# A Mamba scan with side work in hand-chosen slots: half of the pieces stand in other slots

## The chip, the cores and the metric

The kernel runs on one core of one Trainium2 chip. The metric is the device time of one execution in microseconds, as the median of several runs. TensorE is called PE here, VectorE DVE, ScalarE ACT, GpSimd POOL, and SyncE, which issues the DMAs, SP.

## The reference, cut to what matters

A tensor of 8 x 256 x 32 x 32 goes through four layers. The first one is a stack of four Mamba blocks, and the change touches only that; the other three are attention layers. A Mamba block takes the tokens of an image (1024 of 256 channels) and computes:

```python
xn = (xs - mu) * rsqrt(var + 1e-05) * lw + lb
xin, z = split(xn @ iw.T, 2, axis=-1)               # 512 channels each
xin = silu(causal_conv(xin, cw) + cb)               # four taps
proj = xin @ xw.T                                    # 16 for dt, 16 for B, 16 for C
dt = softplus(proj[..., :DTR] @ dw.T + db)
def step(h, t):
    dt_t, b_t, c_t, x_t = t
    h = h * exp(dt_t[..., None] * A) + (dt_t * x_t)[..., None] * b_t[:, None, :]
    return (h, einsum('bdn,bn->bd', h, c_t))         # 16 states a channel
y = ys + xin * dp
xs = xs + y * silu(z) @ ow.T
```

The recurrence over `t` has a state of 512 x 16 values for each image. Everything is float32.

## The kernel before, in words

**Units, steps, slots.** The Mamba phase (`mamba_phase`, L77) cuts the work into 64 units: 4 layers x 8 images x 2 halves of 512 tokens. A unit's scan has 16 steps: two groups `q` of 256 channels, and for each 8 groups `g` of two states. A step has two parts, k = 0 and 1, of 128 channels each. The order of the program is written out by hand. `PARTS` gives it for a step: `ct` (the DMA that spreads C over the partitions, two steps ahead), slot a, `bx0`, `da0`, `y`, `z`, `bx1`, `da1`, slot b, `hc`, slot c, slot d. PE, DVE, ACT and POOL keep this order (class `InOrder`, L40); SP's DMAs are ordered by the scheduler of the framework, which also chooses the buffer of each tile among those of its pool.

What the parts issue:

- `bx0`, `bx1` (`forced` and `state`): 32 matmuls of 64 x 64 on PE form the drive of the recurrence in one of two PSUM buffers `bx`; then DVE runs two scans along the tokens (`TENSOR_TENSOR_SCAN`, the tile `h`). A `bx` buffer is free again when the scans of the part two before have read it.
- `da0`, `da1` (`decays`): ACT computes the decays of the next step, two exponentials each. Eight buffers hold two steps.
- `hc` (`product`): in a first half of the tokens DVE keeps the last column for the second half; POOL multiplies `h` by C.
- `y` (`summed`): PE sums the products of three steps earlier (`LAG_Y`) into PSUM. `z` (`gate`): at the end of a group DVE multiplies the sum by the gate.

**Side work.** The slots a to d carry pieces of other units' work. A unit has 64 slots, four to a step: slot a of step s has number 4s and stands ahead of that step's `bx0`; b, c and d (4s + 1 to 4s + 3) stand behind its `bx1`. On PE the slots 4s + 1 to 4s + 4 lie in one gap between two steps. Five generators hold the side work. `BESIDE_SCAN` says for each which unit it serves, counted from the one that is scanned, and in which slot each of its pieces stands; a slot that stands twice takes two pieces. In a slot the generators are called in the order of the table (`beside`). The pieces are, in order:

- `weights` (two units ahead, in the first unit of a layer only): loads; the exponential of A; a scaled identity; bias matmuls and the scaling of the input weights.
- `onward` (one unit ahead), 16 pieces: `pb`, PE transposes B, ACT copies it to `bt`, and eight small DMAs write it as diagonals to DRAM (`scatter`); then for each of two channel groups the softplus: two matmuls `pd` in two PSUM tiles with two ACT reads each (`e`, `dt`); exponential and `one`; logarithm and `one` again (the logarithm's tile has the tag `sq`, one buffer, which the square of `inward` also has); three POOL additions; the products `dtx` on POOL. The last piece issues nothing.
- `turn` (one unit ahead), 4 pieces: PE transposes `dtx` (`pt`), ACT copies it.
- `outward` (the unit before): load of `xo`; four pieces of output projection on PE (`po`, two tiles, each filled in two pieces), a DVE addition after each tile, and the store. In layer 3 a DVE reduction follows, and after a second half ten more pieces of channel gating (small matmuls `se`, ACT scaling, POOL addition, DVE statistics, loads and stores).
- `inward` (two units ahead), 19 pieces: load of x; mean matmul `pmu` and subtraction on DVE; square on ACT; variance matmul `pvar` with ACT's root; the scaling of `xn` on DVE; then for each of four channel tiles the projection `pin` 0 to 3 with ACT's copy into `xin`, and as a piece of its own three DVE taps of the convolution, which read the same PSUM tile; the gate's projection, `pin` 4 to 7, with ACT's copy `sz`; the SiLU on ACT; and `pp`, the projection to dt, B and C, with its copy and two DMAs.

All of the side work on PE writes PSUM tiles of one pool, `ps_m`, tag `mm`, with two buffers:

```python
ps_b = ctx.enter_context(tc.tile_pool(name="m_psb", bufs=2, space=PSUM))
ps_y = ctx.enter_context(tc.tile_pool(name="m_psy", bufs=1, space=PSUM))
ps_m = ctx.enter_context(tc.tile_pool(name="m_psm", bufs=2, space=PSUM))
```

`DIAGONALS` gives the slots in which a DMA loads one of the next unit's eight diagonals `dg` (L342), which `bx` reads.

Of the kernel before, what the change touches and what calls it, by code (L numbers as in the profile page):

```python
# [52 lines left out]
class Engines:  # L53
# [10 lines left out]
PARTS = ("ct", "a", "bx0", "da0", "y", "z", "bx1", "da1", "b", "hc", "c", "d")  # L64

BESIDE_SCAN = (
    ("weights", 2, (2, 2, 3, 4)),
    ("onward", 1, (3, 5, 8, 12, 12, 13, 21, 25, 27, 31, 35, 35, 41, 46, 46, 51)),
    ("turn", 1, (49, 51, 55, 57)),
    ("outward", -1, (6, 12, 16, 18, 21, 29, 31, 32, 39, 43, 50, 51, 55, 55, 61)),  # L70
    ("inward", 2, (2, 4, 7, 10, 16, 21, 23, 25, 28, 34, 40, 40, 44, 44, 44, 46, 49, 59, 63)),
)

DIAGONALS = (16, 20, 36, 40, 44, 48, 52, 56)


def mamba_phase(tc, ctx, a, spill, ident, gvec, stats):  # L77
# [90 lines left out]
    def out_weights(l, w):  # L168
        w["out"] = wp.tile([P, DT, C], F32, name=f"wo{l}", tag="wo")
        nc.sync.dma_start(w["out"], a["m_out"][l])  # L170
# [171 lines left out]
    def diagonal(s):  # L342

        g = len(s["dg"])
        dg = dgp.tile([P, NB, H, NG], F32, name=f"dg{s['name']}_{g}", tag="dg")
        nc.sync.dma_start(dg, s["dgd"][g * 2 * HALF:(g + 1) * 2 * HALF].rearrange("(p b t j) -> p b t j", p=P, b=NB, t=H))
        s["dg"].append(dg)
# [146 lines left out]
    def beside(n, slot):  # L494

        for what, d, when in BESIDE_SCAN:
# [7 lines left out]
            if slot == when[-1]:  # L504
                for _ in side.pop(what):
                    pass
                if what == "turn" and "out" not in s["w"]:
                    out_weights(s["l"], s["w"])
        if slot in DIAGONALS and 0 <= n + 1 < len(units):
            diagonal(units[n + 1])  # L510
# [609 lines left out]
```

## Time and profile before

| | us |
|---|---|
| median of 3 runs (9191.63 to 9198.40) | 9197.91 |
| the profiled execution, its own time | 9194.97 |
| its span, first to last instruction | 9193.1 |
| PE busy with matmuls, share of the span | 8829.2, 96% |
| DVE busy | 7154.2, 78% |
| POOL busy | 7009.5, 76% |
| ACT busy | 5369.8, 58% |
| mean granted PE clock | 0.975 |

The Mamba phase takes the first 6540 us, some 71% of the span; the rest is attention. In the steady part of the scan, from 211.41 to 6248.59 us, PE is busy 5883.7 us of 6037.2, POOL 5588.2, DVE 5441.1, ACT 4231.0.

In the profile a line names what an instruction writes and reads: `bx<-dg,dtxT` is a matmul that writes `bx`. Nearly all instructions of this phase bear line 48, that of the helper that records them, so they are told apart by their tiles. A float32 matmul shows as two records. An answer on waits says which engine sat idle before which work, and whose end released it. The windows say for a stretch of time how long each engine was busy and which clock PE was granted.

### The profile page before, as it was taken

Reading aid. Unit: us, or ns where it says so; the run is one execution under the profiler, and the core shown is the slowest. Engines: PE = TensorE matmul, PEld = TensorE weight load, DVE = VectorE, ACT = ScalarE, POOL = GpSimd, SP = SyncE. Lnnn points to the kernel's source line nnn. Section 1 sums busy time; section 2 is a strip of 40 time slices with the busy share of each in tenths; the row PEclk is TensorE's granted clock in tenths of the full one; section 3 lists DMA queues with packets and bytes.
Section 4 is the critical chain, followed back from the end, with each engine's and each line's share of the span. In section 5 each row is a group of like instructions: output and inputs, shape, how many; then the busy total and the mean of one; then the engine's idle time right before and its main releaser. Section 6 shows DMA issues by size and latency. Waiting matters only on the chain.

```text
span 9193.1 us, 231133 instructions
## 1 busy us (share of the span) xinstructions
PE 8829.2 (96%) x100850; PEld 4513.2 (49%) x100850; DVE 7154.2 (78%) x7267; ACT 5369.8 (58%) x7646; POOL 7009.5 (76%) x2696
## 2 busy tenths in 40 slices
PE   8999999999999999999999999999799999999998
PEld 4555555555555555555555555555344334434433
DVE  5898988889888898989889999999654554455455
ACT  6667676766776676676667677767323333333334
POOL 5999999999999999999999999999414343343436
PEclk8999999999999999999999999999999999999999
DMA  3434434443443444344444444444200000000000
GB/s 108 129 120 122 124 122 127 121 127 122 122 122 124 127 121 127 122 122 123 123 127 121 137 134 134 135 130 141 99 1 5 10 10 5 5 5 5 1 5 10
DMA packets 559192, 845.58 MB, mean 92 GB/s; under 512 B 311456, under 2 KB 312544, under 8 KB 557536
## 3 DMA queue, kind: packets, MB, share of 16 engines
q1 hardware_dynamic: 558176, 830.71, 29.6%
q8 instruction: 799, 13.09, 0.6%
q14 instruction: 217, 1.78, 0.1%
HBM read 771.31 MB, written 59.24 MB: 90 GB/s over the span
## 4 chain that ended last, share of the span: by engine, by line
PE 86%; DVE 6%; ACT 3%; POOL 2%; issue 2%; DMA 0%; SPq 0%; ACTq 0%; DVEq 0%; POOLq 0%
PE bx L48 20%; PE y L48 19%; PE pin L48 10%; PE fs L655 6%; PE po L48 5%; PE fo L671 4%; DVE h L48 3%; PE fo L759 3%; PE pp L48 3%; PE fs L735 3%; PE pd L48 2%; PE fwq L615 2%; PE fwv L637 2%; PE ft L753 1%; PE pvar L48 1%
## 5 line engine op out<-in xcount | busy, mean ns | idle before, releaser
L48 POOL TENSOR_TENSOR h<-h,ct 128x2048 f32<-128x2048 f32 x1024 | 4640.3, 4544 | 451.9 <-PE y L48 161.3
L48 ACT ACTIVATE da<-dt,A 128x512 f32<-128x512 f32 x4096 | 2642.6, 713 | 224.9 <-DVE h L48 222.6
L48 DVE TENSOR_TENSOR_SCAN h<-da,hc,bx 128x512 f32<-128x512 f32 x2048 | 2456.8, 1261 | 238.8 <-PE bx L48 228.4
L48 DVE TENSOR_TENSOR_SCAN h<-da,bx 128x512 f32<-128x512 f32 x2048 | 2356.9, 1203 | 281.1 <-PE bx L48 266.3
L48 PEld LDWEIGHTS bx<-dg,dtxT 64*64 64x64 f32 x65536 | 1915.0, 135 | 1264.1 <-issue 1178.1
L48 PE MATMUL bx<-dg,dtxT 64*64 64x128 f32 x65536 | 2253.4, 276 | 39.7 <-DVE h L48 28.8
L48 PE MATMUL y<-h,twin 64*64 64x512 f32 x16384 | 2018.8, 608 | 6.1 <-POOL h L48 6.1
L660 ACT ACTIVATE fp<-fs 128x1024 f32<-128x1024 f32 x768 | 765.6, 1022 | 1426.3 <-PE fs L655 1398.0
L48 PE MATMUL pin<-xn,win 128*128 128x512 f32 x2048 | 1009.2, 616 | 61.4 <-ACT sz L48 49.4
L48 PEld LDWEIGHTS y<-h,twin 64*64 64x64 f32 x16384 | 616.1, 138 | 675.6 <-issue 665.8
L677 POOL TENSOR_TENSOR fz<-fz,fp 128x1024 f32<-128x1024 f32 x192 | 478.1, 2490 | 414.5 <-ACT fp L660 410.5
L677 DVE TENSOR_TENSOR fz<-fz,fp 128x1024 f32<-128x1024 f32 x384 | 531.8, 1385 | 328.0 <-ACT fp L660 323.7
L655 PE MATMUL fs<-fq,fk 32*128 32x512 f32 (+1 forms) x3072 | 718.0, 646 | 54.9 <-ACT fp L741 39.3
L48 DVE SCALAR_TENSOR_TENSOR xin<-pin,vec,xin 128x509 f32<-128x509 f32 (+2 forms) x768 | 571.6, 744 | 100.3 <-ACT xin L48 42.8
L671 PE MATMUL fo<-fp,fv 128*32 128x512 f32 (+1 forms) x3072 | 596.6, 615 | 0.0
L48 PEld LDWEIGHTS pin<-xn,win 128*128 128x128 f32 x2048 | 355.6, 191 | 457.9 <-issue 330.4
L48 ACT ACTIVATE xin<-pin,cb,vec 128x512 f32<-128x512 f32 x256 | 199.2, 778 | 621.8 <-PE pin L48 621.8
L48 PE MATMUL po<-sz,wo 128*128 128x512 f32 x1024 | 500.7, 612 | 0.0
L48 ACT ACTIVATE sz<-pin,ib 128x512 f32<-128x512 f32 x256 | 175.9, 687 | 549.8 <-PE pin L48 549.8
L655 PEld LDWEIGHTS fs<-fq,fk 32*128 32x128 f32 (+1 forms) x3072 | 195.3, 185 | 467.8 <-issue 271.0
L677 POOL TENSOR_TENSOR fz<-fp,fp 128x1024 f32<-128x1024 f32 x32 | 83.1, 2597 | 403.2 <-PE fzs L688 240.8
L48 ACT ACTIVATE e<-pd,vec 128x512 f32<-128x512 f32 x256 | 176.1, 688 | 317.4 <-PE pd L48 312.5
(391 smaller groups left out, 8743.4 us busy)
## 6 DMA issues: line engine op xcount, KB each, us to landing
ct<-cdr SPq DMA_DIRECT2D x1024, 512.0 KB, 3.9
dg<-diagonals SPq DMA_DIRECT2D x512, 256.0 KB, 4.3
spill<-xo SPq DMA_DIRECT2D x72, 512.0 KB, 5.3
x<-spill SPq DMA_DIRECT2D x48, 512.0 KB, 7.8
xo<-spill SPq DMA_DIRECT2D x48, 512.0 KB, 5.0
x<-in_x SPq DMA_DIRECT2D x16, 512.0 KB, 8.4
res<-in_x SPq DMA_DIRECT2D x16, 512.0 KB, 5.1
diagonals<-bt SPq DMA_DIRECT2D x512, 4.0 KB, 4.6
```

Source lines behind the costliest of these rows:

```text
L48: return self.tc.keep_in_program_order(getattr(self.engine, name)(*args, **kwargs))
L615: nc.tensor.matmul(ps, lhsT=wt[:, k, m * P:(m + 1) * P], rhs=x[:, k, half * T:(half + 1) * T], start=(k == 0), stop=(k == CT - 1))
L637: nc.tensor.matmul(ps[:, j, :], lhsT=x[:, kc, (t + j) * P:(t + j + 1) * P], rhs=w[f"wv{n}"][:, kc, :], start=(kc == 0), stop=(kc == CT - 1))
L655: nc.tensor.matmul(scs[h // 2][:, h % 2, :], lhsT=k[r:r + D, m, kt * P:(kt + 1) * P], rhs=q[r:r + D, m, half * T:(half + 1) * T], start=Tr ...
L660: nc.scalar.activation(p, scs[j], AF.Exp, scale=scale)
L671: nc.tensor.matmul(acc["o"][r:r + D, :], lhsT=v[:, kt, m * P + r:m * P + r + D], rhs=ps[h // 2][:, h % 2, :], start=(kt == 0), stop=(kt == ...
L677: add(acc["z"][j], acc["z"][j] if kt > 1 else probs[i - 1][j], ps[j], ALU.add)
L735: nc.tensor.matmul(sc[:, half, :], lhsT=q[:, m, t * P:(t + 1) * P], rhs=x[:, m, half * T:(half + 1) * T], start=(m == 0), stop=(m == CT - 1))
L753: nc.tensor.matmul(ps[:, j, :], lhsT=p[:, kt * P:(kt + 1) * P], rhs=dg, start=True, stop=True)
L759: nc.tensor.matmul(po[:, m, :], lhsT=v[:, kt, m * P:(m + 1) * P], rhs=pt[:, kt, :], start=(kt == 0), stop=(kt == TT - 1))
```

## The change

Only the slots change. No instruction is added or taken away: the same pieces of the same generators stand in other slots of a unit.

```diff
 BESIDE_SCAN = (
-    ("weights", 2, (2, 2, 3, 4)),
-    ("onward", 1, (3, 5, 8, 12, 12, 13, 21, 25, 27, 31, 35, 35, 41, 46, 46, 51)),
-    ("turn", 1, (49, 51, 55, 57)),
-    ("outward", -1, (6, 12, 16, 18, 21, 29, 31, 32, 39, 43, 50, 51, 55, 55, 61)),
-    ("inward", 2, (2, 4, 7, 10, 16, 21, 23, 25, 28, 34, 40, 40, 44, 44, 44, 46, 49, 59, 63)),
+    ("weights", 2, (0, 2, 2, 7)),
+    ("onward", 1, (1, 3, 6, 8, 8, 16, 21, 25, 27, 31, 35, 35, 41, 45, 46, 51)),
+    ("turn", 1, (46, 49, 56, 58)),
+    ("outward", -1, (6, 13, 16, 20, 23, 30, 32, 33, 37, 41, 48, 50, 53, 53, 61)),
+    ("inward", 2, (0, 0, 3, 10, 15, 19, 19, 29, 29, 34, 40, 43, 44, 44, 44, 46, 49, 59, 63)),
 )
 
-DIAGONALS = (16, 20, 36, 40, 44, 48, 52, 56)
+DIAGONALS = (12, 20, 36, 40, 44, 48, 52, 56)
```

Read by pieces, the moves with work on PE are these: `pb` from slot 3 to 1 and the first pair of `pd` from 5 to 3 (`onward`); `pmu` from 4 to 0, `pin` 0 from 21 to 19, `pin` 1 from 25 to 29, `pin` 3 from 40 to 43 (`inward`; the taps of `pin` 0 move from 23 to 19, of `pin` 1 from 28 to 29, those of `pin` 2 and 3 stay in 40 and 44); the halves of `po` from 12, 16, 18, 21 to 13, 16, 20, 23; the four `pt` from 49, 51, 55, 57 to 46, 49, 56, 58. Without work on PE: the square from 7 to 3, the scaling of `xn` from 16 to 15; the first group's exponential from 8 to 6, its logarithm from 12 to 8, its POOL additions from 12 and 13 to 8 and 16; the second group's last addition from 46 to 45. The second pair of `pd` stays in slot 27, `pin` 2 in 34, `pin` 4 to 7 in 44, 44, 46 and 49, `pp` in 63.

## The prediction

> **What bounds the kernel now.** I read the busy shares of the page first, then the waits of PE, then the timeline of one unit on PE, and last the clock window by window. The waits, where the columns are the idle time in all, how often, and the longest:
>
> ```profile
> PE pd L48 <- ACT dt L48: 89.5, 63, 1.7
> PE pin L48 <- ACT sz L48: 49.4, 64, 0.8
> ...
> PE bx L48 <- DVE h L48: 28.8, 69, 1.4
> ```
>
> In the scan PE is busy without a break except for these. From the start of unit 1 to the start of unit 61 (211.41 to 6248.59 us) there are 6037.2 us, 100.6 us a unit; PE is idle for 153.5 us of it, 2.56 us a unit: 1.42 before `pd`, 0.78 before `pin`, 0.30 before `bx`. VectorE is busy for 5441 us of that stretch and GpSimd for 5588, so both stand within 10% of PE. The first of the waits looks like this in one unit (start, duration, work, idle time before it):
>
> ```profile
> 3065.09 1.98 PE L48 MATMUL pin<-xn,win 128*128 128x512 f32 x4
> 3067.00 1.12 PE L48 MATMUL pd<-proj,wdt 16*128 16x512 f32 x2
> 3069.53 1.12 PE L48 MATMUL pd<-proj,wdt 16*128 16x512 f32 x2 [1.42 <-ACT dt L48]
> 3070.59 1.90 PE L48 MATMUL bx<-dg,dtxT 64*64 64x128 f32 x32
> 3072.24 2.84 PE L48 MATMUL y<-h,twin 64*64 64x512 f32 x16
> ```
>
> The second `pd` waits until ScalarE has read the first one. And what follows the wait is slower than elsewhere: `bx` takes 1.90 us for what takes 1.10 in other steps, `y` 2.84 for 1.90. The windows around it say why. Columns: length, busy us of PE, PEld, DVE, ACT, POOL, then the granted clock, DMA share and GB/s.
>
> ```profile
> 3063.90:3067.31 3.41, 3.41 (x41) 1.78 (x34) 3.38 (x5) 1.10 (x3) 3.25 (x4) 1.00 0.51 185
> 3067.31:3070.73 3.42, 2.00 (x8) 0.44 (x10) 3.38 (x4) 1.88 (x4) 3.42 (x3) 1.00 0.19 44
> 3070.73:3074.14 3.41, 3.41 (x44) 2.24 (x45) 2.38 (x4) 3.41 (x6) 3.41 (x2) 0.50 0.82 268
> 3074.14:3077.55 3.41, 3.41 (x88) 2.31 (x84) 2.44 (x3) 3.38 (x5) 1.86 (x1) 1.00 0.14 31
> 3091.21:3094.62 3.41, 2.63 (x7) 1.02 (x6) 3.41 (x5) 0.69 (x1) 3.41 (x1) 1.00 0.09 29
> 3094.62:3098.03 3.41, 3.41 (x51) 1.58 (x53) 3.34 (x5) 2.51 (x5) 3.41 (x3) 1.00 0.62 176
> ```
>
> The window with the 1.42 us of idle time is followed by one at half clock; the one with the 0.78 us before `pin` (fifth line) is not. I laid all clock records of the scan on this grid of 3.41 us: in units 1 to 60 there are 60 stretches at half clock, 279.9 us in all (38 of one window, 22 of two), nearly all beginning within 2.2 us of the second `pd`. Of the windows of the whole trace with 1.4 to 1.5 us idle 56 of 58 were followed by half clock, of those with 0.7 to 0.8 none of 65. So the wait costs twice: 1.42 us, and 279.9 / 2 / 60 = 2.33 us a unit for matmuls at half speed. Together 3.75 us of 100.6.
>
> [...]
>
> **The change part by part.** Times are from the start of a unit's first `bx`, medians over 16 units from the timelines.
>
> *The second delta pair.* Before, `pin` 1 (slot 25, read by VectorE until slot 28) held one bank when the two `pd` of slot 27 came, so both got the other: in the built order the pair shares a bank in 63 units of 63. After, `pin` 1 comes in slot 29, and the pair shares a bank in 1 unit. Each then waits for readers that are long done: the first for `pin` 0's, at about 31 us, the second for the `xo` addition at about 36.5, while PE arrives at 39. This takes away 1.42 + 2.33 = 3.75 us a unit. What is late next stands below.
>
> *`pin` 1 and its taps in slot 29.* VectorE now works off the three taps (2.22 us without overlap) after step 7, and `pin` 2's at slot 40 after step 9; step 9 has no side work on PE behind it. Let E be the end of `pin` 1. ScalarE's copy lets the taps begin at E + 0.9 (before: `pin` 0 ends at 37.08, taps at 37.98). Then 2.22 for the taps, 4.69 for step 8 (26.72 to 31.41 in a step without a wait), 2.33 for the first two scans of step 9, and 0.1 to PE: E + 10.2. PE, unhindered, needs step 8 (3.63), `pin` 2 (1.91) and step 9 without side work (3.53) and wants that `bx` buffer at E + 9.0. **A new wait of 1.2 us before `bx` of step 10**, each unit. Bounds: 0 if VectorE's chain is shorter than I laid it, 2.0 where VectorE comes in late, as in layer 3, where a reduction of 1.22 us is added at slot 23.
>
> Does that trip the clock? Windows with only `bx` and `y`:
>
> ```profile
> 6415.78:6419.19 3.41, 1.66 (x41) 1.23 (x39) 2.75 (x4) 3.27 (x6) 3.41 (x2) 1.00 0.11 36
> 6419.19:6422.60 3.41, 2.78 (x48) 1.43 (x48) 1.15 (x2) 0.25 (x1) 3.41 (x2) 1.00 0.56 195
> 6477.22:6480.63 3.41, 2.06 (x65) 1.65 (x61) 3.41 (x4) 1.45 (x2) 3.08 (x1) 1.00 0.47 183
> 6480.63:6484.05 3.42, 2.89 (x60) 1.65 (x52) 3.42 (x4) 2.17 (x3) 1.75 (x1) 1.00 0.75 225
> ```
>
> Idle times of 1.75 and 1.35 us there left the clock at 1.00; 2.12 (at 6443 us) did not. With `pd`, which fills 16 of 128 rows, 1.09 was enough and 1.04 was not. So 1.2 us before a `bx` should leave it.
>
> *`pb` and the first delta pair (slots 3, 5 to 1, 3).* They now follow each other on PE, and the second `pd` takes `pb`'s bank: a new wait for ScalarE's copy `bt`. Queued behind it on PE are the `bx` of step 1, and so VectorE. Before, `bt` ended 1.08 us after `pb` (5.12 against 4.04), since ScalarE was still at decays. After, `pmu` (1.92 us) stands ahead on PE while ScalarE's row of work from `pt` 3 is the same 12.0 us plus its copy, 12.6 in all, against 13.05 on PE to the end of `pb`: ScalarE is there first, `bt` ends 0.25 us after `pb`, and the first `pd` covers 0.53. I take 0; upper bound 1.08 - 0.53 = 0.6.
>
> *`pmu` and subtraction to slot 0, square to 3.* The matmul and the 1.2 us of VectorE lie beside `pp` and cost nothing: VectorE stands at about -2 then. The load of x is issued a unit ahead in SP's order in both kernels, now before the eight writes of the diagonals rather than after them; the next `ct` behind them needs 3.9 us to land and has two products of 4.5 us on GpSimd as cover.
>
> *Logarithm to slot 8.* It shares a buffer with the square, so on ScalarE it now waits for the `pvar` matmul, and the decays of step 3 queue behind it. `pvar` ends near 14.2; logarithm and identity take 2.1, the first decay is there at 17.0; VectorE wants it at 17.35. Cost 0, and up to 0.3 on VectorE, which has 2.8 us before PE asks for that buffer.
>
> *GpSimd's sums (12, 13, 46 to 8, 16, 45).* The sum of its work is 16 x 4.50 + 14.2 + 5.0 + 2.0 = 93.2 us a unit, under 98. Laid in the new order, its products end 2.3 us or more before their `y`. Cost 0; without that cover the first late one would be step 12's.
>
> *The rest.* `po` 0 and 1 in slots 13, 16, 20, 23, the transposes in 46, 49, 56, 58 and `pin` 3 in 43 are the same matmuls beside the same steps; `pin` 4 and 5 share a bank in 63 units as before, so 0.78 stays. The first diagonal moves from slot 16 to 12, but stands directly behind the writes in SP's order in both. The weights' pieces act in 4 units of 64. I take 0 for all.
>
> *Sum.* A unit: 100.6 - 3.75 + 1.2 = 98.1. Gain 2.55 x 62 units = 158 us; less 0.8 x 13 units of layer 3, and a half-clock window in some of them (13 x 0.9), 22 us together: 136. The profiled execution took 9194.97 us (span 9193.1), 2.9 under the median of 9197.91. 9194.97 - 136 = 9059, with 3 us to the median 9062; the start, where matrix sums no longer stand behind the weights' load (8.9 us of waiting), should give some back: **9055**.
>
> **The rivals.** (A) The new waits trip the clock once a unit as the old one did: 98.1 + 2.33 = 100.4, 13 us gained in all, 9185. For it: the fit of two windows to a threshold is thin. Against: the lines above. 0.10. (B) Slower: the second `pd` of slot 3 waits for `bt` because ScalarE doesn't get ahead. [...] 98.1 + 1.1 + 2.33 = 101.5, 0.9 x 62 = 56 us lost, 9250. For it: 1.08 us of lag before. Against: `pmu` on PE ahead of it. 0.08. (C) The new VectorE wait doesn't come: 96.9 a unit, 62 x 1.2 more gained, 8980. 0.10. That the bank conflict stays is excluded by the built order (1 of 63).
>
> **How the numbers follow.** The likeliest case, 9055 with 8990 to 9120 (new wait 0.6 to 1.8 us), has 0.72. The range of 8965 to 9160 adds (C) and leaves out (B) and most of (A). About 0.2% (18 us) is what a measurement of this kernel can tell from no change. Faster by more than that: 0.72 + 0.10 + 0.03 of (A) = 0.85; within: 0.07; slower: 0.08.
>
> **What would show it.** Right: no wait of `pd` on `dt`, a mean clock above 0.98, no half-clock window a unit, waits of `bx` on `h` of some 60 to 80 us instead of 28.8, `pin` on `sz` still near 49. Wrong: half-clock windows behind `bx` of step 10 (A), waits of `pd` on `bt` (B), or waits of `y` on GpSimd's `h`, which would mean that GpSimd, not VectorE, is late next.

## The result, and the profile after

The kernel after took **8987.25 us** (median of 4 runs, 8978.97 to 8989.28) against 9197.44 for the kernel before (4 runs, 9191.63 to 9198.40). The ratio is 0.9771, with a 95% interval of 0.9754 to 0.9788: 210 us gained, where 142 were forecast. The time lies in the forecast range of 8965 to 9160, but 68 us under its number, 9055, and 3 us under the 8990 that bounded its likeliest case. The profiled execution took 8988.71 us, its span 8986.9, and the mean granted clock is 0.990 (before: 0.975).

The waits of PE after, by the same view as before (idle time in all, how often, the longest):

```profile
PE bx L48 <- DVE h L48: 93.0, 134, 4.9
PE pin L48 <- ACT sz L48: 49.7, 65, 0.8
...
PE pd L48 <- ACT dt L48: 2.2, 1, 2.2
```

The 89.5 us of `pd` on `dt` are 2.2, from one occurrence; the wait of `pin` on `sz` is what it was; `bx` waits for VectorE 93.0 us instead of 28.8. Here are the second delta pair and the new wait in one unit (start, duration, work, idle time before it):

```profile
3066.03 1.13 PE L48 MATMUL pd<-proj,wdt 16*128 16x512 f32 x4
3067.09 1.10 PE L48 MATMUL bx<-dg,dtxT 64*64 64x128 f32 x32
3068.01 1.90 PE L48 MATMUL y<-h,twin 64*64 64x512 f32 x16
...
3083.06 1.10 PE L48 MATMUL bx<-dg,dtxT 64*64 64x128 f32 x32 [1.00 <-DVE h L48]
```

Three things are to be seen. The four records of the pair stand together and take 1.13 us, as much as *two* of them took before (1.12). The `bx` and `y` behind them take 1.10 and 1.90 us, and the granted clock is 1.00 from 3066.20 to 3069.62. And `bx` of step 10 waits 1.00 us. The clock windows around the new wait (length, busy us of PE, PEld, DVE, ACT, POOL, then clock, DMA share, GB/s):

```profile
3079.87:3083.28 3.41, 2.41 (x55) 1.45 (x49) 3.38 (x5) 3.38 (x6) 3.41 (x2) 1.00 0.15 55
3083.28:3086.69 3.41, 3.41 (x81) 2.25 (x73) 3.34 (x5) 2.77 (x5) 3.41 (x3) 1.00 0.57 196
```

The first has the 1.00 us of idle time, the next one is at clock 1.00.

From the start of unit 1 to that of unit 61 there are now 5832.3 us, 97.21 a unit (before 100.62). PE is idle in 138.3 us of it (before 153.5): 85.8 before `bx`, 46.7 before `pin`, none before `pd`. Half-clock stretches are left at the three layer changes alone, 13.7 us where there were 279.9 in all (6.8 of them at layer changes). So a unit gained 3.41 us, of which only 0.25 is idle time; the rest, 98.06 less 94.90 = 3.16 us, is time in which PE was busy before. Half clock explains (279.9 - 13.7) / 2 / 60 = 2.22 of it, an estimate that takes half of the time at clock 0.50 as lost. **What the other 0.94 are, my sum had no term for**, and this is what the experiments went after.

### The profile page after: what moved, and what is told of

Same layout as the page of the kernel before. It is cut to its first block, busy times and chain, and to the rows that moved or that the text cites. A ratio compares the mean times of both kernels' runs of the same rounds, so it can differ in the third digit from the quotient of the medians.

```text
span 8986.9 us, 231646 instructions
## 1 busy us (share of the span) xinstructions
PE 8635.8 (96%) x100850; PEld 4454.0 (50%) x100850; DVE 7164.6 (80%) x7267; ACT 5375.6 (60%) x7646; POOL 6999.4 (78%) x2696
## 4 chain that ended last, share of the span: by engine, by line
PE 80%; DVE 11%; ACT 3%; issue 3%; POOL 2%; DMA 1%; SPq 0%; POOLq 0%; DVEq 0%; ACTq 0%
PE bx L48 17%; PE y L48 16%; PE pin L48 9%; DVE h L48 8%; PE fs L655 6%; PE po L48 5%; PE fo L671 5%; PE fo L759 3%; PE fs L735 3%; PE pp L48 3%; PE fwq L615 2%; PE fwv L637 2%; PE pd L48 2%; PE pvar L48 1%; PE ft L753 1%
## 5 line engine op out<-in xcount | busy, mean ns | idle before, releaser
L48 PEld LDWEIGHTS bx<-dg,dtxT 64*64 64x64 f32 x65536 | 1886.6, 133 | 1303.3 <-issue 1048.8
L48 PE MATMUL bx<-dg,dtxT 64*64 64x128 f32 x65536 | 2224.0, 273 | 119.7 <-DVE h L48 93.0
L48 PE MATMUL y<-h,twin 64*64 64x512 f32 x16384 | 1958.3, 591 | 4.8 <-POOL h L48 4.8
L48 PE MATMUL pin<-xn,win 128*128 128x512 f32 x2048 | 991.6, 612 | 64.5 <-ACT sz L48 49.7
L48 POOL TENSOR_TENSOR e<-e,one 128x1024 f32<-128x1024 f32 x128 | 303.7, 2372 | 78.6 <-ACT one L48 78.6
```

The source lines that it names most:

```text
L48: return self.tc.keep_in_program_order(getattr(self.engine, name)(*args, **kwargs))
```

## The experiments

Unless another number of runs is given, each was timed with four executions beside the kernel before, whose median was 9190.8 to 9195.4 us. A unit means the mean of units 1 to 60.

**Only `pin` 1 moved**: the kernel before with

```diff
-    ("inward", 2, (2, 4, 7, 10, 16, 21, 23, 25, 28, 34, ...
+    ("inward", 2, (2, 4, 7, 10, 16, 21, 23, 29, 29, 34, ...
```

> The kernel before with one move alone: pin 1 and its taps from slots 25 and 28 to 29 and 29. In the built order the second pair of pd no longer shares a bank (1 unit of 63), all other pieces stand as before. Bank theory: the wait (1.42 us), the half clock (2.2 us) and the lost overlap of the two pd (about 1.0 us) go in each of some 61 units, and pin 3 stays in slot 40, so that the gap on PE behind step 9 is filled and no wait of bx on h of 1 us appears: 9197 - 4.6 x 61 = about 8915. Rival, that the changed kernel gains from all of its moves together: this one move gives at most half of the 210 us, about 9090 or more.

Measured: 9001.89 us (9000.27 to 9006.15), ratio 0.979 [0.9774, 0.9806]. So one of the many moves carries 193 of the 210 us. PE is busy 94.94 us a unit, as in the kernel after, and half clock is down to 13.7 us: the gains came in full. But the time is 87 us above the 8915 that I expected, for there is a new wait of PE in front of step 7, 56.7 us in all, where I had expected none:

```profile
2973.15 1.13 PE L48 MATMUL pd<-proj,wdt 16*128 16x512 f32 x4
2975.22 1.10 PE L48 MATMUL bx<-dg,dtxT 64*64 64x128 f32 x32 [0.95 <-PE pd L48]
```

The releaser named there is PE's own `pd`, which had ended 0.94 us before. VectorE's timeline at the same time shows the real one:

```profile
2970.44 2.32 DVE L48 SCALAR_TENSOR_TENSOR xin<-pin,vec,xin 128x509 f32<-128x509 f32 x3 [1.29 <-ACT xin L48]
2972.68 8.30 DVE L48 TENSOR_TENSOR_SCAN h<-da,hc,bx 128x512 f32<-128x512 f32 x7
```

The scans of step 6 begin at 2972.68 and the second of them, which frees the `bx` buffer, ends about 2975.1. I took the idle time of 1.29 us at the head of the taps of `pin` 0, ahead of these scans, for the cause of the lateness; that isn't shown, and the last experiment doesn't settle it. In the kernel before, the taps have the same 1.29 us, but PE stood before `dt` then, and the lateness cost nothing.

**Only `pin` 1 left where it was**: the kernel after with

```diff
-    ("inward", 2, (0, 0, 3, 10, 15, 19, 19, 29, 29, 34, ...
+    ("inward", 2, (0, 0, 3, 10, 15, 19, 19, 25, 28, 34, ...
```

> The changed kernel with pin 1 and its taps put back to slots 25 and 28, all other moves kept. The pair of pd shares a bank again in 63 units. Bank theory: wait, half clock and lost overlap return (4.6 us a unit), the new wait of bx on h (1.0 us) goes: 8987 + 3.6 x 61 = about 9205, level with before. Rival, that the other moves carry part of the gain: clearly under before, 9100 or less.

Measured (9 runs): 9224.09 us (9211.08 to 9239.76), ratio 1.0028 [1.0018, 1.0038]. The wait before the second `pd` is back with 85.3 us in these units, half clock with 273 us. All the other moves together, without this one, make the kernel 0.28% slower: PE is busy as long as before (98.07 a unit) and idle 0.48 us longer; of these 29 us in 60 units, 24 are before `bx` of step 10.

**Both `pd` of a pair on the same rows**: the kernel after with

```diff
-                nc.tensor.matmul(pds[r], lhsT=w["dt"][r * H:r * H + DTR, i * P:(i + 1) * P], rhs=tokens(proj[r * H:r * H + DTR, :]),
+                nc.tensor.matmul(pds[r], lhsT=w["dt"][:DTR, i * P:(i + 1) * P], rhs=tokens(proj[:DTR, :]),
```

The rows 64 to 79 hold a second copy of the same projection and of the same weights, made so that the two `pd` of a pair, which differ in their channels, can stand on different rows. So the values stay what they are, and the work is the same in number and shape.

> The changed kernel with both pd of a pair on the same 16 rows, so that they run one after the other instead of side by side; they compute the same. Nobody waits for a bank. Overlap term: 0.95 us for each of two pairs a unit, 8987 + 2 x 0.95 x 61 = about 9103. If only idle time trips the clock, it stays at full speed in all but some 3 windows; if rows count, [...] some units may lose up to 2 us more (up to 9200). If the overlap is worth nothing: level with 8987.

Measured: 9039.17 us (9033.13 to 9049.25), ratio 0.9834 [0.9818, 0.985]; 52 us slower than the kernel after, half of what I expected. The second pair, which took 1.13 us:

```profile
2110.84 1.98 PE L48 MATMUL pd<-proj,wdt 16*128 16x512 f32 x4
2112.75 1.00 PE L48 MATMUL bx<-dg,dtxT 64*64 64x128 f32 x28
```

From `pd` to `bx` there are 1.91 us instead of 1.06. That is the missing term: a `pd` on rows 0 to 15 and one on rows 64 to 79 of PE ran side by side in the kernel after, 1.06 us against 1.91 on the same rows. Before, with one bank (one buffer of `ps_m`) for the pair, they couldn't, since the second `pd` waited 1.42 us until ScalarE had read the first. The other half of my expectation failed because the *first* pair lost only 0.16 us: it took long already. In the kernel after, it stands directly behind `pb`, whose bank the second `pd` takes (PE, and then ScalarE's copy `bt` of that bank):

```profile
2057.80 0.23 PE L48 MATMUL pb<-ident,proj 16*128 16x16 f32 x1
2057.81 0.69 PE L48 MATMUL pd<-proj,wdt 16*128 16x512 f32 x1
2057.89 0.33 PE L48 MATMUL pb<-ident,proj 16*128 16x16 f32 x3
2058.35 1.29 PE L48 MATMUL pd<-proj,wdt 16*128 16x512 f32 x3
2059.57 1.10 PE L48 MATMUL bx<-dg,dtxT 64*64 64x128 f32 x32
```

```profile
2058.26 0.21 ACT L48 COPY bt<-pb 128x64 f32<-128x64 f32 x1 [0.77 <-PE pb L48]
```

The copy ends at 2058.47, and the second `pd`, two of the three records in the fourth line, starts at 2058.52, 0.71 us behind the first one. In the second pair it starts 0.01 us behind.

**The first pair in slot 5, behind step 1**, tried on the kernel after and on the faster kernel with the taps moved that comes further down (5 runs each):

```diff
-    ("onward", 1, (1, 3, 6, 8, 8, ...
+    ("onward", 1, (1, 5, 6, 8, 8, ...
```

> The kernel after with the first delta pair in slot 5 in place of slot 3, nothing else changed. By the theory of the lost overlap PE is 0.34 us earlier a unit from step 2 on, but the wait for VectorE before bx of step 10, 1.00 us now, may take up part of it, as it took up nothing when the same pair was made slower by 0.16 us: VectorE there is fed by PE's own steps. All of it kept: 8987 - 21 = 8966. All of it taken up by that wait: 8987, with the wait at 1.34.

> This is the kernel with the taps of pin 2 and pin 3 in slots 37 and 40 (8943 us), and besides the first delta pair is moved from slot 3 to slot 5, behind step 1, with pb left in slot 1. The theory is that the kernel after lost the side-by-side running of its first pair: behind step 0, PE needs 1.70 us for pb and the two pd (3.69 to 5.39 in a unit), where pb adds 0.3 and a pair that overlaps 1.06, together 1.36. The second pd stands in pb's bank and starts only when bt has been copied, by which time the first one is nearly through. In slot 5, the copy is long done, the pair overlaps, and 0.34 us a unit come back, 62 x 0.34 = 21 us: 8922. The rival: the 1.70 us have another cause (pb is dearer than I take it), or VectorE, which is needed for bx of step 2, takes up what PE saves: within 8 us of 8943.

Measured: 8973.40 us (8962.51 to 8978.08), ratio 0.9755 [0.9742, 0.9768], on the kernel after, and **8920.75 us** (8917.41 to 8930.50), ratio 0.9705 [0.9691, 0.9718], on the other, where 8922 was expected. In the first, `pb` is alone and the pair runs in 1.13 us:

```profile
2055.38 0.42 PE L48 MATMUL pb<-ident,proj 16*128 16x16 f32 x4
2055.73 1.10 PE L48 MATMUL bx<-dg,dtxT 64*64 64x128 f32 x32
...
2059.36 1.13 PE L48 MATMUL pd<-proj,wdt 16*128 16x512 f32 x4
2060.50 1.10 PE L48 MATMUL bx<-dg,dtxT 64*64 64x128 f32 x32
```

In ordinary units `bx` of step 2 starts 8.73 us into the unit instead of 9.10 in one half of the units and 9.22 in the other: on average 0.43 us, which is what the slots 1 and 3 cost. The wait before step 10 stays at 1.00 us, so it takes up nothing of this. Ordinary units gain 25 us together; that only 14 us came is at the three layer changes, whose units got 9.7 us longer together, for a reason that I didn't follow up.

**The delta matmuls over all rows**: the kernel before, with zeros in the weight's other rows.

```diff
-        w["dt"] = wp.tile([H + DTR, DI], F32, name=f"wdt{l}", tag="wdt")
-        for r in range(2):
-            nc.sync.dma_start(w["dt"][r * H:r * H + DTR, :], a["m_dt"][l])
+        w["dt"] = wp.tile([XP, DI], F32, name=f"wdt{l}", tag="wdt")
+        nc.gpsimd.memset(w["dt"], 0.0)
+        nc.sync.dma_start(w["dt"][:DTR, :], a["m_dt"][l])
...
-                nc.tensor.matmul(pds[r], lhsT=w["dt"][r * H:r * H + DTR, i * P:(i + 1) * P], rhs=tokens(proj[r * H:r * H + DTR, :]),
+                nc.tensor.matmul(pds[r], lhsT=w["dt"][:, i * P:(i + 1) * P], rhs=tokens(proj),
```

The zeros meet all rows but the first copy of the projection, so dt is what it was.

> The kernel before with pd over 112 rows instead of 16: its weights are padded with zeros, all else stands, the bank conflict too. Theory of rows: [...] the wait stays and the half-clock windows go: 9197 - 2.2 x 61 = 9062, plus 0.95 x 61 for the first pair of pd, which can no longer run side by side: about 9120, up to 9160 where VectorE falls behind. Rival, that the idle time alone decides: some 60 half-clock windows remain, 9197 + 58 = about 9255.

Measured: 9132.74 us (9126.20 to 9138.77), ratio 0.993 [0.9913, 0.9946], clock 0.990. A unit's second pair, and the windows it stands in:

```profile
2634.98 1.02 PE L48 MATMUL pd<-proj,wdt 112*128 112x512 f32 x2
2637.42 1.13 PE L48 MATMUL pd<-proj,wdt 112*128 112x512 f32 x2 [1.42 <-ACT dt L48]
2638.48 1.10 PE L48 MATMUL bx<-dg,dtxT 64*64 64x128 f32 x32
```

```profile
2635.90:2639.31 3.41, 1.99 (x34) 1.13 (x36) 3.34 (x5) 2.05 (x5) 3.41 (x4) 1.00 0.42 106
2639.31:2642.73 3.42, 3.27 (x76) 1.95 (x72) 3.32 (x4) 3.42 (x6) 3.42 (x2) 1.00 0.58 206
```

The wait is there to the hundredth, the window has the same 1.42 us of idle time, and the next is at clock 1.00. Of the 40 windows in units 1 to 60 with 1.4 to 1.5 us idle beside a `pd`, none is followed by half clock, where before it was 51 of 51; half clock in these units falls from 279.9 to 37.5 us, all of it at the layer changes or in the unit behind them. So the idle time alone didn't decide it here: the same pause of 1.42 us was followed by half clock beside the matmuls of 16 rows (51 of 51) and not beside the padded ones (none of 40). From the first `pd` to `bx` there are 3.50 us, less the wait 2.08, against 1.06 after: one behind the other, the pair takes 1.02 us more. The first pair, which is no longer side by side either, takes 1.91 instead of 1.06, and the units at the layer changes and behind them are 26 us longer together, where `pd` waits for its padded weights (13.8 us in all); so the kernel gains little.

**The second pair split**: the kernel before with the two `pd` of each pair as pieces of their own, those of the second in slots 27 and 29, each read by ScalarE at once. Of the edit, the slots are shown; the rest splits the piece in `onward`.

```diff
-    ("onward", 1, (3, 5, 8, 12, 12, 13, 21, 25, 27, 31, 35, 35, 41, 46, 46, 51)),
+    ("onward", 1, (3, 5, 5, 8, 12, 12, 13, 21, 25, 27, 29, 31, 35, 35, 41, 46, 46, 51)),
```

> The kernel before with the second pair of pd pulled apart: the first in slot 27, the second in slot 29, each with its own two reads, and one more piece in the list for it; pin 1 stays in 25 and 28. They still share a bank, but between them lies step 7 on PE, so nobody waits. Wait and half clock go, the overlap of the two pd does not come back (each takes 1.06 us alone). If the gain has the three terms 1.42, 2.2 and 1.0 us: 9197 - 3.6 x 61 = about 8975, some 60 us above the run in which only pin 1 moves. If the overlap is worth nothing, the two are level; if the wait itself was all and the clock nothing, about 9110.

Measured: 9118.68 us (9116.62 to 9126.25), ratio 0.9915 [0.9898, 0.9931]: a miss by 144 us. The wait for `dt` is gone, but a wait for VectorE stands behind the second `pd`, and the windows show what it does:

```profile
3033.44 1.12 PE L48 MATMUL pd<-proj,wdt 16*128 16x512 f32 x2
3035.88 1.87 PE L48 MATMUL bx<-dg,dtxT 64*64 64x128 f32 x32 [1.32 <-DVE h L48]
```

```profile
3032.65:3036.06 3.41, 2.09 (x41) 1.12 (x37) 3.41 (x4) 2.50 (x5) 3.41 (x2) 1.00 0.71 233
3036.06:3039.47 3.41, 3.41 (x44) 2.34 (x43) 3.41 (x4) 3.38 (x5) 2.98 (x2) 0.50 0.16 64
```

The 1.32 us idle beside a `pd` of 16 rows are followed by clock 0.50, as the old wait was, in 42 of 60 units (half clock is 167.1 us in all). A unit's busy time of 97.09 us is that of the kernel after, 94.90, with 1.28 for half clock (beyond what that kernel has) and a remainder of 0.91. It fits two `pd` that don't overlap, and comes near the 0.94 that I was looking for.

**Filling the pause before step 10**: the kernel after, with the taps of `pin` 2 in slot 37 instead of 40, and `pin` 3 in slot 40 instead of 43.

```diff
-    ("inward", 2, (0, 0, 3, 10, 15, 19, 19, 29, 29, 34, 40, 43, 44, 44, 44, ...
+    ("inward", 2, (0, 0, 3, 10, 15, 19, 19, 29, 29, 34, 37, 40, 44, 44, 44, ...
```

> The changed kernel with the taps of pin 2 in slot 37 and pin 3 in slot 40 instead of 40 and 43, so that PE has 1.9 us of side work behind step 9, where it now waits 1.0 us for VectorE in each unit. If the wait there is only a matter of what PE has to do meanwhile: 8987 - 61 x 1.0 = about 8925, and bx waits on h fall from 93 us to some 30. Rival, that VectorE is the bound of this stretch and the wait returns at a later step: within 15 us of 8987.

Measured: **8942.95 us** (8934.99 to 8946.56), ratio 0.9726 [0.9709, 0.9742]. The wait before step 10 is gone, `bx` waits on VectorE 37.6 us in all instead of 93.0, and the wait does not return at a later step, as it would if VectorE's sum of work were the bound: given `pin` 3 to do there, PE comes when VectorE is ready. The gain came to 44 us and not 62, since PE's busy time rose by 0.15 us a unit (95.05), which I didn't follow up.

**The same for the pause before `pin` 5**, on top of that: the taps of `pin` 3 in slot 44 are as they were, `pin` 5 goes to slot 45.

```diff
-    ("inward", 2, (0, 0, 3, 10, 15, 19, 19, 29, 29, 34, 37, 40, 44, 44, 44, 46, ...
+    ("inward", 2, (0, 0, 3, 10, 15, 19, 19, 29, 29, 34, 37, 40, 44, 44, 45, 46, ...
```

> The changed kernel with the taps of pin 2 in slot 37, pin 3 in slot 40 and pin 5 in slot 45 instead of 44, so that it no longer follows pin 4, whose bank it takes. The wait of pin on sz (0.78 us a unit) goes; pin 6 now waits some 0.25 us behind pin 5 and pt. From the run with the first two moves (8943): - 0.5 x 61 = about 8912. Rival, that VectorE is behind at step 11 once PE comes 2.7 us earlier, and bx waits in its place: within 12 us of 8943.

Measured: 8958.46 us (8944.46 to 8964.71), ratio 0.9745 [0.9729, 0.9761], no gain, nearer to the rival (level within 12 us of 8943) than to my 8912, and 15 us slower than that kernel. `pin` waits 22.6 us instead of 49.7 and `bx` 57.2 instead of 37.6: the pause was covering VectorE.

**`pin` 0 two slots earlier beside `pin` 1** (5 runs): the kernel before with

```diff
-    ("inward", 2, (2, 4, 7, 10, 16, 21, 23, 25, 28, 34, ...
+    ("inward", 2, (2, 4, 7, 10, 16, 19, 19, 29, 29, 34, ...
```

> The kernel before with pin 1 and its taps in slot 29, and pin 0 and its taps in slot 19 (before: 21 and 23), nothing else. With pin 1 alone it took 9002 us, and PE waited 0.95 us before bx of step 7 in each unit. In the trace of that kernel VectorE has worked off step 5 and the addition, and then sits idle for 1.29 us at the head of the taps of pin 0 until ScalarE's copy of pin 0 is there, with the scans of step 6, whose bx is ready, queued behind them. The theory: that is the whole wait before step 7. With pin 0 two slots earlier the copy is done when VectorE gets there, and the wait goes: 0.9 x 62 = 56 us, 8946. What may stand against it is that VectorE, no longer late at step 7, meets the wait before step 10 that the kernel after has (1.00 us where this kernel had 0.41 at step 9): then 0.6 x 62 = 37 us of it come back, 8983. The rival, that VectorE's backlog at step 7 is its sum of work and not that idle time: 9002, with the wait where it was.

Measured: 9011.65 us (9005.17 to 9013.55), ratio 0.98 [0.9787, 0.9814], no gain over `pin` 1 alone. In the first three layers the wait at step 7 falls from 0.88 and 0.95 us, in every other unit, to 0.36 and 0.53, and doesn't go; the idle time at the head of these taps moved with them, and is still 1.0 us. And in layer 3 the wait at step 7 grows to 1.6 to 1.8 us in 12 units, 20.4 us in all, 10 of them with half clock behind; units there take up to 101.2 us. So this run neither bears out that the idle time is the whole wait nor excludes it: the idle time wasn't taken away. What it shows is that a slot that helps one stage can trip another.

## Why the prediction was right, and where its size was off

**The bank conflict** (step "the second delta pair"): right. The wait of 1.42 us a unit is gone, and the kernels with `pin` 1 alone moved and alone left show that this one move does it.

**The clock**: right. 2.33 us a unit were forecast, 2.22 came; the difference is the 13.7 us of half clock that the layer changes have after. The full-row experiment shows that the halving came from the pause together with the narrow matmuls (none of 40 such windows with the padded ones, 51 of 51 with those of 16 rows).

**The term that was mis-sized** is in the same step. "This takes away 1.42 + 2.33 = 3.75 us a unit" counts the wait and the clock and leaves the matmuls themselves at what they took. Without the wait, from the first `pd` to `bx`, they took 2.17 us at full clock (in the unit of the prediction 3070.59 - 3067.00 - 1.42) and take 1.06 side by side: 1.11 us a unit more, or 69 us over 62 units, where the full-row kernel has 1.02 a unit. The profile of before showed it, had I compared its two pairs: the second is two groups of 1.12 us, and the first, in different banks, is one group of four records:

```profile
3033.96 1.13 PE L48 MATMUL pd<-proj,wdt 16*128 16x512 f32 x4
```

**`pb` and the first pair**: forecast at 0, with 0.6 as the bound. The wait for `bt` is there, but hardly as idle time (0.7 us in the whole trace), since the first `pd` covers it. It costs the overlap of the pair instead, 0.43 us a unit, which was inside the bound.

**The new wait before step 10**: right in place and cause, 1.00 us instead of 1.2. `pin` 1 ends at 45.85 us into the median unit; `bx` starts at 56.21, which is E + 10.36 where I had E + 10.2. PE was ready at E + 9.36 rather than 9.0. A wait of 0.13 before step 9 and 0.04 elsewhere come with it.

**The sum.** A unit, forecast: -1.42 - 2.33 + 1.20 = -2.55. Measured: -1.42 - 2.22 + 1.00 + 0.17 for the waits and the clock, -1.11 and +0.43 for the two pairs, which makes -3.15 of the -3.41. Where the last 0.26 come from stays open. A hint is that the kernel with `pin` 1 alone moved, whose first pair runs side by side, keeps PE busy as long (94.94 against 94.90): so the other moves save about what they cost at the first pair, and which of them does wasn't tried.

**Layer 3**: 0.8 us a unit more, as forecast (97.55 against 96.75), but without the half-clock windows that I had added (12 us).

**The other moves** at nothing each: together they gain 15 us on `pin` 1 alone and lose 27 without it. A sum of zeros was too simple: without `pin` 1 the loss is idle time before `bx`, that is, VectorE coming late; with it, PE is idle 9.5 us less in units 1 to 60, and what the first pair loses is won elsewhere. GpSimd plays no part: `y` waits for its `h` 4.8 us in the whole trace.

**The rivals.** (A), the new waits trip the clock: it didn't come. 58 windows at full clock in the trace after have 0.9 to 1.1 us idle, and none is followed by half clock. The split pair shows that the danger was real: there 1.32 us beside a `pd` were followed by clock 0.50. (B), a wait for `bt` with half clock: not as a wait, and that the clock would halve there was my estimate alone. (C), no new wait: refuted by 93.0 us, though its 8980 lies nearest; the right time would have been for the wrong reason. That the measured time fell into the range is in part luck: it lies in the part below 8990 that I had added for (C), and what brought it there was the overlap of the pair, for which I had no term.

## What to carry to other kernels

When two matmuls on different rows are meant to run side by side, look whether their records stand together. Here the second waited for the readers of a PSUM bank that the two shared, and the price was the wait (1.42 us a unit), the time of a further matmul (1.11), and the clock (2.22), and only the first is called a wait in the profile. Before you take a wait away, look who else is late under it: here VectorE's lateness came out at step 7, 8 or 10, by kernel (0.95, 1.32 and 1.00 us), as soon as PE no longer waited, and one piece of work for PE at the right slot (`pin` 3 in slot 40, with the taps of `pin` 2 moved out of its way) was worth 44 us more. With the first pair moved as well, 8921 us is the best of the kernels here.

## What was not expected of the hardware

In the kernel before, a window of 3.41 us with a pause of 1.42 us beside matmuls on 16 rows was followed by half clock (51 of 51 windows with 1.4 to 1.5 us idle in units 1 to 60). In the kernel with the split pair 1.32 us beside one of them were (clock 0.50 from 3036.06 us on). With the same matmuls filled up with zeros to 112 rows the pause of 1.42 us was not (none of 40, mean clock 0.990 against 0.975). Part of a window was enough, and the padding of the matmuls in the rest of it made the difference.

The trace of before gives no single idle time from which on it happened. Beside 1.12 to 2.00 us of `pd`, in units 1 to 60, all 58 full-clock windows with 1.09 to 1.42 us idle were followed by half clock, and the one with 0.88 (at 4780.81 us) was not, nor one with 1.04 behind these units (at 6292.91). But two ahead of unit 1, with 1.03 us idle beside 2.24 us of `pd` and 1.05 beside 1.33 (at 63.59 and 121.61), were. The 1.04 against 1.09 of the prediction is one window each. Whether it is the number of rows as such that counts, or something else that the padding changed, two row counts can't tell; that it is the rows was my estimate.
